# Moving ELU's sums and the residual of a graph attention layer from VectorE to GpSimd, with a second head's product moved the other way

## The chip, the cores and the metric

One Trainium2 chip, one core of it. A core has TensorE (matrix products into PSUM; PE in the profile, its weight loads PEld), VectorE (DVE), ScalarE (ACT), GpSimd (POOL) and SyncE (SP), which here only issues DMAs. The engines run side by side and wait for one another through semaphores. The metric is the device time of one execution in microseconds (us); lower is better.

## The reference

Two layers over 4096 nodes with 512 features. Layer 0 is dense attention with the adjacency matrix added to the logits. Layer 1 is graph attention with 8 heads of 64 features, and is the part that is edited:

```python
h = relu(layernorm(x))
nX = (h @ W).reshape(n, 8, 64).transpose(1, 0, 2)        # per head, then normalised over its 64 features
at1, at2 = nX . a1, nX . a2                              # one number per head and node
kg = leaky_relu(at1[i] + at2[j], 0.2) * adj[i, j]
attention = softmax(where(adj[i, j] != 0, kg, -32768), over j)
y = attention @ nX + nX
x = x + elu(y)
```

`elu(y)` is y where y is positive, and exp(y) - 1 elsewhere.

## The kernel before

Layer 0 runs first, to about 2090 us of the profile, and is not edited. Layer 1 works in groups: 8 chunks of 512 destination nodes i, times 2 halves of the heads (4 heads at a time), so 16 groups. A group has 32 steps, one for each block of 128 source nodes j; the 512 steps run in one loop, and the order of the instructions on every compute engine is written out by hand (`seq`). The DMA issues of SP that matter here are in that order too.

What one step n issues, in this order:

- `values(n - 4)`, TensorE, L996: the weighted sums of an earlier step, from the exponentials `t` into `acc` (PSUM), for 4 heads.
- `exponent(n - 3)`, ScalarE, L983: exp over the 4 heads of `t`, 2048 elements per partition.
- `leaky(n)`, VectorE: for two of the four heads a maximum and a sum from PSUM (L969 twice), for head 3 the product with the graph's values `g` (L973), and for heads 0 and 1 a sum with PSUM (L974).
- `weigh(n)`, GpSimd, L980: the product with `g` for the other three heads, 1536 elements per partition.
- `z_sums(n + 1)`, TensorE, L948 and L953: the logits of the next step, into PSUM tiles `d`, of which there are three.
- `relu(n + 1)`, ScalarE, L960: from PSUM to `t`.

`t` has six buffers. So GpSimd works on the step that VectorE has just left, or on an earlier one, and VectorE can run some steps ahead of it; the text calls this distance VectorE's lead.

SP issues the loads. Every fourth step `load_adj` brings `z2`, `nb` and `g` for the four steps after the running ones; `g` has two buffers, so its issue (L900) waits until GpSimd has finished the last product that read the older one, and everything behind it on SP waits too. `open_group` (L913, L916) loads `z1` and `u4` of the next group, four steps before that group begins, which puts it behind the `load_adj` of the same step. `load_rows` loads the residual `xi` and the rows `own` of a group at its step 12; there is one buffer of each.

The end of a group is spread over steps of the next one, counted from the step in which the group's last `values` run (`finish`): copies of `acc` on ScalarE at +0; transposes on TensorE at +1 and +2, each followed on VectorE by `divide` (L1027 to L1032), which also keeps the least and greatest sum in `low` and `high` for a flag at the very end; `minus` on ScalarE at +4 and +5; `exps` on ScalarE at +6 and +7; then, both on VectorE, `elu` (L1050) at +9 and `close` (L1054) at +10, which adds the residual and stores the result (L1058).

Of the kernel before, what the change touches and what calls it, by code (L numbers as in the profile page):

```python
# [10 lines left out]
F32 = mybir.dt.float32  # L11
# [7 lines left out]
P = 128  # L19
# [59 lines left out]
def fast_path(  # L79
# [45 lines left out]
    HB = HD + 1  # L125
    back = const.tile([P, 2, HB], F32, name="back")

    low = const.tile([P, 2, 4], F32, name="low")
    high = const.tile([P, 2, 4], F32, name="high")
    low0 = const.tile([P, SB], F32, name="low0")  # L130
    high0 = const.tile([P, SB], F32, name="high0")
    for t in (low, high, low0, high0):
        nc.vector.memset(t, 1.0)


# [742 lines left out]
    with tc.tile_pool(name="ga_in", bufs=2) as inputs, tc.tile_pool(  # L878
# [4 lines left out]
        JB = 4  # L883
        STEPS = [(ic, hg, jt) for ic in range(NI) for hg in range(NH // HG) for jt in range(NB)]
        n_steps = len(STEPS)
        loads, logits, zs, groups = {}, {}, {}, {}
        later = {}

        def load_adj(q):
# [19 lines left out]
        def open_group(n, queue):  # L909

            ic, hg, _ = STEPS[n]
            z1 = inputs.tile([P, GC], BF16, name="z1", tag="z1", bufs=2)
            seq(queue.dma_start(out=z1, in_=z1_d[:, hg, ts(ic, GC)]))  # L913
            u4 = inputs.tile([P, 2, GC], F32, name="u4", tag="u4", bufs=2)
            for e in range(2):
                seq(queue.dma_start(  # L916
                    out=u4[:, e, :].rearrange("p (b i) -> p b i", i=P),
                    in_=u4_d[ic * SB : (ic + 1) * SB, hg * HG + 2 + e, :]
                    .unsqueeze(0).to_broadcast([P, SB, P]),
                ))  # L920
            groups[ic, hg] = {"z1": z1, "u4": u4}
# [41 lines left out]
        def leaky(n):  # L963

            ic, hg, jt = STEPS[n]
            t, pair, u4 = logits[n], zs.pop(n), groups[ic, hg]["u4"]
            for e in (1, 0):
                h = hg * HG + 2 + e
                seq(nc.vector.scalar_tensor_tensor(  # L969
                    pair[1][:, 1, :] if e else t[:, 2, :], u4[:, e, :], at2m[:, jt, h : h + 1],  # L970
                    pair[1][:, e, :], ALU.max, ALU.add,
                ))
            seq(nc.vector.tensor_mul(t[:, 3, :], pair[1][:, 1, :], loads[n // JB][0][:, jt % JB, :]))  # L973
            seq(nc.vector.tensor_add(t[:, 0:2, :], t[:, 0:2, :], pair[0]))  # L974

        def weigh(n):

            g = loads[n // JB][0][:, STEPS[n][2] % JB, :].unsqueeze(1).to_broadcast([P, 3, GC])
            t = logits[n]
            seq(nc.gpsimd.tensor_mul(t[:, 0:3, :], t[:, 0:3, :], g))  # L980

        def exponent(n):
            seq(nc.scalar.activation(logits[n], logits[n], AF.Exp))  # L983
# [17 lines left out]
        def finish(n, ic, hg):  # L1001

            grp = groups.pop((ic, hg))
            ob = work.tile([P, 2, GC], F32, name="ob", tag="ob", bufs=1)
            y = work.tile([P, 2, SB * 2, HD], F32, name="y", tag="y", bufs=1)

            def room():
                grp["e"] = work.tile([P, 2, SB * 2, HD], F32, name="e", tag="ob", bufs=1)

            def copies():  # L1010
                for hf in range(2):
                    seq(nc.scalar.copy(ob[:, hf, :], grp["acc"][hf]))

            def to_rows(hf):
                pt = psum.tile([P, 2, GC], F32, name="pt1", tag="d", bufs=3)
                for b in range(SB):
                    col = (b % 2) * 2 * HB
                    seq(nc.tensor.matmul(  # L1018
                        pt[:, b // 2, col : col + 2 * HB], ob[:, hf, ts(b, P)],
                        back.rearrange("p e c -> p (e c)"), start=True, stop=True,  # L1020
                    ))
                grp["pt"] = pt[:, :, 0 : 4 * HB].rearrange("p k (q c) -> p k q c", c=HB)

            def divide(hf):
                v = grp.pop("pt")
                rinv = work.tile([P, 2, 4], F32, name="rinv1", tag="rinv1", bufs=2)
                seq(nc.vector.reciprocal(rinv, v[:, :, :, HD]))  # L1027
                seq(nc.vector.tensor_tensor(low, low, v[:, :, :, HD], ALU.min))
                seq(nc.vector.tensor_tensor(high, high, v[:, :, :, HD], ALU.max))
                v = v[:, :, :, 0:HD]  # L1030
                seq(nc.vector.tensor_mul(v, v, rinv.unsqueeze(3).to_broadcast([P, 2, 4, HD])))  # L1031
                seq(nc.vector.tensor_add(  # L1032
                    y[:, hf].rearrange("p (k q) e -> p k q e", k=2), v,
                    grp["own"][:, hf].rearrange("p b d -> p (b d)")
                    .rearrange("p (k q e) -> p k q e", k=2, e=HD),
                ))

            def flat(t):
                return t.rearrange("p f q e -> p (f q e)")

            def minus(hf):
                seq(nc.scalar.activation(grp["e"][:, hf], y[:, hf], AF.Relu, scale=-1.0))

            def exps(hf):
                e = grp["e"][:, hf]
                seq(nc.scalar.activation(e, e, AF.Exp, scale=-1.0))

            def elu():
                e = flat(grp["e"])
                seq(nc.vector.scalar_tensor_tensor(e, e, -1.0, flat(y), ALU.add, ALU.max))  # L1050

            def close():
                e = grp["e"]
                seq(nc.vector.tensor_add(  # L1054
                    flat(e), flat(e), grp["xi"].rearrange("p f b d -> p (f b d)")
                ))
                for f, ap in enumerate(pair_rows(out, ic, hg)):
                    nc.sync.dma_start(  # L1058
                        out=ap, in_=e[:, f].rearrange("p (b h) e -> p b (h e)", h=2)
                    )  # L1060

            for d, place, f in (
                (0, "mid", copies),
                (1, "mid", lambda: to_rows(0)), (1, "end", lambda: divide(0)),
                (2, "mid", lambda: to_rows(1)), (2, "end", lambda: divide(1)),
                (4, "end", room), (4, "end", lambda: minus(0)), (5, "end", lambda: minus(1)),
                (6, "end", lambda: exps(0)), (7, "end", lambda: exps(1)),
                (9, "end", elu), (10, "end", close),
            ):
                later.setdefault((n + d, place), []).append(f)  # L1070
# [34 lines left out]
        for n in range(n_steps + 15):  # L1105

            q = n // JB + 1
            if n == 1:
                store_rows(NI - 1, last_rows)
            if n % JB == (2 if q == NS - 1 else 0) and q < n_steps // JB:  # L1110
                load_adj(q)
                if q < NS:
                    load_features(q)
            if n < n_steps and STEPS[n][2] == 12:
                load_rows(n)
            if n + 4 < n_steps and STEPS[n + 4][2] == 0:
                open_group(n + 4, nc.sync)
            extra(n, "top")
            if 0 <= n - 4 < n_steps:
                values(n - 4)  # L1120
                if n % JB == 3:
                    loads.pop((n - 4) // JB)
                if STEPS[n - 4][2] == NB - 1:
                    finish(n, *STEPS[n - 4][:2])
            if 0 <= n - 3 < n_steps:
                exponent(n - 3)
            extra(n, "mid")
            for f in left.pop(n, []):
                f()
            if n % JB == 2 and n // JB < NS:  # L1130
                ones_in(n // JB)
            if n < n_steps:
                leaky(n)
                weigh(n)
            if n + 1 < n_steps:
                z_sums(n + 1)
                relu(n + 1)
            for f in left_late.pop(n, []):
                f()
            extra(n, "end")  # L1140
# [1 line left out]

        ends = work.tile([P, 4], F32, name="ends", tag="ends", bufs=1)
        nc.vector.tensor_reduce(ends[:, 0:1], low0, AX.X, ALU.min)
        nc.vector.tensor_reduce(ends[:, 1:2], low, AX.XY, ALU.min)
        nc.vector.tensor_reduce(ends[:, 2:3], high0, AX.X, ALU.max)
        nc.vector.tensor_reduce(ends[:, 3:4], high, AX.XY, ALU.max)
        good = work.tile([P, 4], F32, name="good", tag="good", bufs=1)
        nc.vector.tensor_scalar(good[:, 0:2], ends[:, 0:2], TINY, None, ALU.is_ge)
        nc.vector.tensor_scalar(good[:, 2:3], ends[:, 2:3], HUGE0, None, ALU.is_le)  # L1150
        nc.vector.tensor_scalar(good[:, 3:4], ends[:, 3:4], HUGE1, None, ALU.is_le)
        pl = psum.tile([4, P], F32, name="pl", tag="d", bufs=3)
        nc.tensor.transpose(pl, good, ident)
        worst = work.tile([4, 1], F32, name="worst", tag="worst", bufs=1)
# [409 lines left out]
```

## Time and profile before

| | |
|---|---|
| time, median of 3 runs | 4024.99 us (4022.72 to 4026.66) |
| the profiled execution | 4015.42 us, span 4013.6 us, mean clock of TensorE 0.982 |
| busy, share of the span | PE 95%, DVE 73%, ACT 44%, POOL 64% |
| GpSimd's product L980 | 512 instructions, 1783.5 us, 3517 ns each |
| VectorE's `elu` sum L1050 | 16, from 1226 to 6367 ns, median 1952 |
| VectorE's residual sum L1054 | 16, 1218 to 1232 ns |
| ScalarE's exponent L983 | 512 instructions, 974.4 us, 1903 ns each |

The shares are means over two layers with different limits: in layer 1 the product on GpSimd takes most of its time, in layer 0 GpSimd is idle for much of it. In the timeline, two columns of numbers stand ahead of the engine: the start and the duration; what stands in brackets at the end of a line is how long the engine was idle before it, and what ended that. A duration can overlap the next instruction's start by some 0.1 us, so the pace is read from start to start.

### The profile page before, as it was taken

What the parts mean: (1) busy time and instruction counts of PE and PEld (TensorE: products, weight loads), DVE (VectorE), ACT (ScalarE), POOL (GpSimd) and SP (SyncE); (2) the same over time, 40 slices, a digit from 0 to 9 for tenths busy, and PEclk for the clock granted to TensorE, in tenths of its full rate; (3) what the DMA queues carried; (4) which work ended last, traced back from release to release, by engine and by line L of the source; (5) the groups of instructions that cost most, each with busy time, mean ns of one, the idle gap of its engine ahead of it and who ended that gap; (6) DMA issues with size and microseconds to landing.
All of it is one profiled execution on the core that took longest, in us unless ns stands there. A gap on an engine that the chain in (4) does not pass through costs nothing. (4 is left out here: it accounts for less than half of the span.)

```text
span 4013.6 us, 43955 instructions
## 1 busy us (share of the span) xinstructions
PE 3810.1 (95%) x15217; PEld 1801.6 (45%) x15370; DVE 2921.6 (73%) x4425; ACT 1752.9 (44%) x1549; POOL 2552.0 (64%) x1249
## 2 busy tenths in 40 slices
PE   8989999999999999999988899999999999999997
PEld 4446666666666666666642222222222222222222
DVE  5445556565565656565556899999999999999997
ACT  1000011111111111111115787887778877877887
POOL 3432125252342525243357899999999999999998
PEclk9999999999999999999989999999999999999999
DMA  6466657667685857667565544444444444444442
GB/s 214 173 213 197 202 161 216 188 180 219 187 220 167 226 171 209 199 184 222 153 194 146 154 134 140 141 140 139 137 139 131 144 139 131 135 136 136 136 139 88
DMA packets 554407, 670.37 MB, mean 167 GB/s; under 512 B 79808, under 2 KB 397504, under 8 KB 534720
## 3 DMA queue, kind: packets, MB, share of 16 engines
q1 hardware_dynamic: 552112, 665.70, 55.7%
q8 instruction: 122, 2.00, 0.2%
q10 hardware_dynamic: 2064, 1.77, 0.2%
q14 instruction: 109, 0.89, 0.1%
HBM read 495.12 MB, written 172.23 MB: 166 GB/s over the span
## 5 line engine op out<-in xcount | busy, mean ns | idle before, releaser
L980 POOL TENSOR_TENSOR t<-t,g 128x1536 f32<-128x1536 f32 x512 | 1783.5, 3517 | 108.9 <-DVE t L974 85.4
L996 PE MATMUL acc<-t,nX 128*64 128x512 f32 x4096 | 1022.3, 621 | 20.3 <-ACT t L983 12.9
L739 POOL TENSOR_TENSOR total<-total,aT 128x512 f32<-128x512 f32 x248 | 339.7, 1370 | 1061.3 <-ACT aT L734 1054.8
L983 ACT ACTIVATE t<-t 128x2048 f32<-128x2048 f32 x512 | 974.4, 1903 | 3.0 <-POOL t L980 3.0
L749 PE MATMUL acc<-v,aT 128*128 128x512 f32 x2048 | 962.7, 593 | 0.0
L734 ACT ACTIVATE aT<-aT 128x512 f32<-128x512 f32 x256 | 161.2, 630 | 1325.0 <-DVE aT L729 1317.0
L960 ACT ACTIVATE t<-d 128x1024 f32<-128x1024 f32 x512 | 525.4, 1026 | 419.0 <-PE d L953 396.3
L974 DVE TENSOR_TENSOR t<-t,d 128x1024 f32<-128x1024 f32 x512 | 619.8, 1211 | 0.0
L953 PE MATMUL d<-nb,ident_b 128*128 128x512 bf16 x1895 | 521.3, 389 | 14.9 <-issue 9.4
L749 PEld LDWEIGHTS acc<-v,aT 128*128 128x128 f32 x2048 | 389.7, 190 | 273.8 <-issue 245.5
L996 PEld LDWEIGHTS acc<-t,nX 128*64 128x64 f32 x4096 | 254.9, 139 | 549.5 <-issue 360.0
L969 DVE SCALAR_TENSOR_TENSOR d<-u,at2m,d 128x512 f32<-128x512 f32 x512 | 383.7, 749 | 87.9 <-PE d L953 41.4
L969 DVE SCALAR_TENSOR_TENSOR t<-u,at2m,d 128x512 f32<-128x512 f32 x512 | 382.4, 747 | 55.2 <-DVE d L969 3.2
L729 DVE TENSOR_TENSOR aT<-aT,X 128x256 f32<-128x256 f32 x512 | 214.9, 420 | 279.2 <-PE X L721 275.8
L948 PE MATMUL d<-z,z 6*128 6x512 bf16 x2048 | 265.0, 388 | 115.6 <-DVE t L973 92.4
L729 DVE TENSOR_TENSOR aT<-aT,Z 128x256 f32<-128x256 f32 x384 | 159.6, 416 | 292.1 <-PE Z L721 287.5
L973 DVE TENSOR_TENSOR t<-d,g 128x512 f32<-128x512 f32 x512 | 349.9, 683 | 0.9 <-DMA g<-gT_d 0.9
L948 PEld LDWEIGHTS <-z 6*128 6x128 bf16 x2048 | 85.4, 91 | 539.6 <-issue 523.3
L713 DVE SCALAR_TENSOR_TENSOR gs<-ng,aT 128x512 f32<-128x512 bf16 x256 | 286.1, 1117 | 9.8 <-DMA gT_d<-gs 1.2
L721 PE MATMUL Z<-qt,hS 128*128 128x256 f32 x1024 | 265.9, 382 | 8.6 <-DVE aT L729 8.4
L953 PEld LDWEIGHTS <-ident_b 128*128 128x128 bf16 x2048 | 160.1, 98 | 246.8 <-issue 128.9
L721 PE MATMUL X<-qt,hT 128*128 128x256 f32 x1024 | 263.8, 380 | 0.5 <-DVE aT L729 0.5
(160 smaller groups left out, 3079.5 us busy)
## 6 DMA issues: line engine op xcount, KB each, us to landing
g<-gT_d SPq DMA_DIRECT2D x128, 1024.0 KB, 5.4
ag<-in_adj_dram SPq DMA_DIRECT2D x256, 256.0 KB, 5.6
hT<-h_d SPq DMA_DIRECT2D x64, 1024.0 KB, 5.9
hS<-s_d SPq DMA_DIRECT2D x64, 1024.0 KB, 8.2
gT_d<-gs SPq DMA_DIRECT2D x256, 256.0 KB, 3.1
nb<-nT_d SPq DMA_DIRECT2D x128, 512.0 KB, 3.3
nT_d<-ng SPq DMA_DIRECT2D x256, 128.0 KB, 3.4
z<-z_d SPq DMA_DIRECT2D x143, 128.0 KB, 2.1
```

Source lines behind the costliest of these rows:

```text
L721: seq(nc.tensor.matmul(out, a, b, start=start and k == 0, stop=k == 1, skip_group_check=not start,))
L729: seq(nc.vector.tensor_add(p, p, part))
L749: seq(nc.tensor.matmul(sums[ic][b], probs[s][:, ts(b, P)], v[:, jt, :], start=jt == 0, stop=jt == NB - 1))
L948: seq(nc.tensor.matmul(pair[hh // 2][:, hh % 2, :], z2[rows, ts(jt % JB, P)], groups[ic, hg]["z1"][rows, :], start=True, stop=False,))
L953: seq(nc.tensor.matmul(pair[hh // 2][:, hh % 2, :], ident_b, ng[:, jt % JB, :], start=False, stop=True))
L960: seq(nc.scalar.activation(t[:, 0:2, :], zs[n][0], AF.Relu, scale=4.0))
L969: seq(nc.vector.scalar_tensor_tensor(pair[1][:, 1, :] if e else t[:, 2, :], u4[:, e, :], at2m[:, jt, h : h + 1], pair[1][:, e, :], ALU.max ...
L973: seq(nc.vector.tensor_mul(t[:, 3, :], pair[1][:, 1, :], loads[n // JB][0][:, jt % JB, :]))
L974: seq(nc.vector.tensor_add(t[:, 0:2, :], t[:, 0:2, :], pair[0]))
L980: seq(nc.gpsimd.tensor_mul(t[:, 0:3, :], t[:, 0:3, :], g))
L983: seq(nc.scalar.activation(logits[n], logits[n], AF.Exp))
L996: seq(nc.tensor.matmul(grp["acc"][hf][ts(e, HD), :], nX[jt // SB][:, jt % SB, hg * HG + 2 * hf + e, :], t[:, 2 * hf + e, :], start=jt == 0 ...
```

## The change

Five things are edited, all in layer 1.

1. `elu` and `close` run on GpSimd. Since GpSimd only adds there, ScalarE prepares both terms: `positive` makes y its positive part after `exps(0)` at +6, and `less_one` subtracts one from the exponentials at +8.
2. In the steps +9 and +10 of 15 groups (the set `light`; the last group has no products left to share) VectorE takes the product of heads 2 and 3, and GpSimd that of heads 0 and 1 alone.
3. `open_group` runs ten steps ahead of a group rather than four.
4. `divide` writes its reciprocals into one tile that is kept, `inverses`, and no longer updates `low` and `high`; the flag is worked out from `inverses` at the end.
5. The tile `inverses` is declared twice; the first declaration is not used.

```diff
+        inverses = gat.tile([P, NI, 2, 2, 2, 4], F32, name="inverses")
+        light = {n + d for n in range(NB + 3, n_steps, NB) for d in (9, 10)}
...
+            mine = 2 if n in light else 1
             for e in (1, 0):
                 h = hg * HG + 2 + e
                 seq(nc.vector.scalar_tensor_tensor(
-                    pair[1][:, 1, :] if e else t[:, 2, :], u4[:, e, :], at2m[:, jt, h : h + 1],
-                    pair[1][:, e, :], ALU.max, ALU.add,
+                    pair[1][:, e, :] if e > 1 - mine else t[:, 2, :], u4[:, e, :],
+                    at2m[:, jt, h : h + 1], pair[1][:, e, :], ALU.max, ALU.add,
                 ))
-            seq(nc.vector.tensor_mul(t[:, 3, :], pair[1][:, 1, :], loads[n // JB][0][:, jt % JB, :]))
+            g = loads[n // JB][0][:, jt % JB, :].unsqueeze(1).to_broadcast([P, mine, GC])
+            seq(nc.vector.tensor_mul(t[:, HG - mine : HG, :], pair[1][:, 2 - mine : 2, :], g))
...
         def weigh(n):
-            g = loads[n // JB][0][:, STEPS[n][2] % JB, :].unsqueeze(1).to_broadcast([P, 3, GC])
+            mine = 2 if n in light else 3
+            g = loads[n // JB][0][:, STEPS[n][2] % JB, :].unsqueeze(1).to_broadcast([P, mine, GC])
             t = logits[n]
-            seq(nc.gpsimd.tensor_mul(t[:, 0:3, :], t[:, 0:3, :], g))
+            seq(nc.gpsimd.tensor_mul(t[:, 0:mine, :], t[:, 0:mine, :], g))
...
-                rinv = work.tile([P, 2, 4], F32, name="rinv1", tag="rinv1", bufs=2)
+                rinv = inverses[:, ic, hg, hf]
                 seq(nc.vector.reciprocal(rinv, v[:, :, :, HD]))
-                seq(nc.vector.tensor_tensor(low, low, v[:, :, :, HD], ALU.min))
-                seq(nc.vector.tensor_tensor(high, high, v[:, :, :, HD], ALU.max))
...
+            def positive():
+                seq(nc.scalar.activation(flat(y), flat(y), AF.Relu))
+            def less_one():
+                seq(nc.scalar.add(flat(grp["e"]), flat(grp["e"]), -1.0))
             def elu():
                 e = flat(grp["e"])
-                seq(nc.vector.scalar_tensor_tensor(e, e, -1.0, flat(y), ALU.add, ALU.max))
+                seq(nc.gpsimd.tensor_add(e, e, flat(y)))
             def close():
                 e = grp["e"]
-                seq(nc.vector.tensor_add(
+                seq(nc.gpsimd.tensor_add(
                     flat(e), flat(e), grp["xi"].rearrange("p f b d -> p (f b d)")
                 ))
...
-                (6, "end", lambda: exps(0)), (7, "end", lambda: exps(1)),
+                (6, "end", lambda: exps(0)), (6, "end", positive), (7, "end", lambda: exps(1)),
+                (8, "end", less_one),
                 (9, "end", elu), (10, "end", close),
...
-            if n + 4 < n_steps and STEPS[n + 4][2] == 0:
-                open_group(n + 4, nc.sync)
+            if n + 10 < n_steps and STEPS[n + 10][2] == 0:
+                open_group(n + 10, nc.sync)
```

More of the change, by code (lines that the diff above doesn't have):

```diff
@@ L126, in fast_path @@
     back = const.tile([P, 2, HB], F32, name="back")
-    low = const.tile([P, 2, 4], F32, name="low")
-    high = const.tile([P, 2, 4], F32, name="high")
     low0 = const.tile([P, SB], F32, name="low0")
     high0 = const.tile([P, SB], F32, name="high0")
-    for t in (low, high, low0, high0):
+    for t in (low0, high0):
         nc.vector.memset(t, 1.0)
@@ L885, in fast_path @@
         n_steps = len(STEPS)
+        inverses = gat.tile([P, NI, 2, 2, 2, 4], F32, name="inverses")
+        inverses = gat.tile([P, NI, 2, 2, 2, 4], F32, name="inverses")
         loads, logits, zs, groups = {}, {}, {}, {}
+        light = {n + d for n in range(NB + 3, n_steps, NB) for d in (9, 10)}
         later = {}
@@ L1144, in fast_path @@
         nc.vector.tensor_reduce(ends[:, 0:1], low0, AX.X, ALU.min)
-        nc.vector.tensor_reduce(ends[:, 1:2], low, AX.XY, ALU.min)
+        of_all = inverses.rearrange("p i g f k q -> p (i g f k q)")
+        nc.vector.tensor_reduce(ends[:, 1:2], of_all, AX.X, ALU.max)
         nc.vector.tensor_reduce(ends[:, 2:3], high0, AX.X, ALU.max)
-        nc.vector.tensor_reduce(ends[:, 3:4], high, AX.XY, ALU.max)
+        nc.vector.tensor_reduce(ends[:, 3:4], of_all, AX.X, ALU.min)
         good = work.tile([P, 4], F32, name="good", tag="good", bufs=1)
-        nc.vector.tensor_scalar(good[:, 0:2], ends[:, 0:2], TINY, None, ALU.is_ge)
+        nc.vector.tensor_scalar(good[:, 0:1], ends[:, 0:1], TINY, None, ALU.is_ge)
+        nc.vector.tensor_scalar(good[:, 1:2], ends[:, 1:2], 1.0 / TINY, None, ALU.is_le)
         nc.vector.tensor_scalar(good[:, 2:3], ends[:, 2:3], HUGE0, None, ALU.is_le)
-        nc.vector.tensor_scalar(good[:, 3:4], ends[:, 3:4], HUGE1, None, ALU.is_le)
+        nc.vector.tensor_scalar(good[:, 3:4], ends[:, 3:4], 1.0 / HUGE1, None, ALU.is_ge)
         pl = psum.tile([4, P], F32, name="pl", tag="d", bufs=3)
```

## The prediction

> **What bounds the kernel now.** I read the page's shares first, then the stretches of layer 1 group by group, then GpSimd's waits, then VectorE, TensorE and SyncE in time around one group's end. The mean shares mislead: they mix layer 0 (to about 2090 us) with layer 1, the rest, and only layer 1 is edited.
>
> ```profile
> 2996.20:3112.46 116.26, 108.07 (x523) 33.03 (x530) 107.23 (x142) 93.11 (x71) 111.82 (x33) 0.99 0.43 137
> 3112.46:3226.10 113.64, 106.46 (x520) 32.94 (x528) 107.12 (x141) 93.11 (x71) 111.75 (x33) 1.00 0.45 140
> 2417.15:3928.80 1511.65, 1413.97 (x6746) 430.70 (x6868) 1401.37 (x1822) 1210.42 (x911) 1456.05 (x421) 0.98 0.44 138
> ```
>
> These are stretches: length, then busy time of PE, PEld, DVE, ACT and POOL. The first two are one group (32 steps) each, cut at the residual sum; the third is thirteen groups, 116.28 us each. GpSimd (POOL) is busiest: 112 us in each group, idle 55.6 us over thirteen, 4.2 us a group. So it is nearly the limit, and its idle time is what can be had without making it faster. Who makes it idle:
>
> ```profile
> POOL t L980 <- DVE t L974: 85.4, 60, 4.4
> DVE d L969 <- DMA u<-u_d: 36.1, 14, 3.5
> PE d L948 <- DVE t L973: 77.7, 51, 6.0
> ```
>
> (The last row is from the steady window of layer 1.) VectorE delivers late, and itself waits 2.6 us at 14 group starts for u4. Now one undisturbed step, and the disturbed ones of the group at 2412 to 2533 us:
>
> ```profile
> 2434.55 0.75 DVE L969 SCALAR_TENSOR_TENSOR t<-u,at2m,d 128x512 f32<-128x512 f32 x1
> 2435.22 0.68 DVE L973 TENSOR_TENSOR t<-d,g 128x512 f32<-128x512 f32 x1
> 2435.82 1.21 DVE L974 TENSOR_TENSOR t<-t,d 128x1024 f32<-128x1024 f32 x1
> 2437.84 44.55 POOL L980 TENSOR_TENSOR t<-t,g 128x1536 f32<-128x1536 f32 x13
> 2469.73 1.43 SPq L916 DMA_DIRECT2D u<-u_d  x2
> 2478.71 0.76 DVE L969 SCALAR_TENSOR_TENSOR d<-u,at2m,d 128x512 f32<-128x512 f32 x1 [2.73 <-DMA u<-u_d]
> 2483.09 2.72 PE L996 MATMUL acc<-t,nX 128*64 128x512 f32 x8
> 2513.90 1.94 PE L996 MATMUL acc<-t,nX 128*64 128x512 f32 x8 [0.24 <-ACT t L983]
> 2526.72 1.95 DVE L1050 SCALAR_TENSOR_TENSOR e<-e,y 128x1024 f32<-128x1024 f32 x1
> 2530.84 0.39 PE L948 MATMUL d<-z,z 6*128 6x512 bf16 x2 [1.55 <-DVE t L973]
> 2531.83 1.22 DVE L1054 TENSOR_TENSOR e<-e,xi 128x1024 f32<-128x1024 f32 x1
> 2532.13 3.36 PE L996 MATMUL acc<-t,nX 128*64 128x512 f32 x8
> ```
>
> VectorE and TensorE repeat every 3.245 us (L969 at 2433.70 and 2436.95). GpSimd repeats every 3.43 us (44.55/13). So VectorE gains 0.19 us of lead per step, 6.1 us in 32, and loses it at the group's end: two divides 3.85 us (2.17 and 1.68), ELU 1.87, residual 1.15, the u4 wait 2.6, and TensorE slow after each gap (acc 2.72 or 3.36 us instead of 1.94). With the lead gone, GpSimd waits.
>
> **What the Trainium skill says.** Its page "SBUF — State Buffer", section "SBUF: two separate sides": a VectorE instruction with two SBUF inputs and a GpSimd one exclude each other on a shared port. The trace agrees: L1050 takes 1.95 us beside GpSimd (5.4 to 6.4 in three of sixteen groups) and 1.23 at the end, where GpSimd is done, and the product beside L1050 or L1054 takes 4.38 instead of 3.44. Other VectorE work of a step reads PSUM, and shows no such stretch. The Trainium skill's "TensorE: Matmul & The Clock Gate", section "What's actually happening": idleness halves TensorE's clock for a while. The trace agrees and is stricter: a gap of 1.55 us was enough (the lines at 2530.84 and 2532.13), one of 0.53 was not.
>
> **The change, part by part.**
>
> *GpSimd.* In 30 steps (15 groups, two each) its product shrinks from 1536 to 1024 elements, and one 1024-element sum follows. A 1024-element operation is not in the trace; from 1.27 us (L351, 512) and 3.44 (1536) it is 2.35 us. The Trainium skill's "GPSIMD Engine Reference", section 3.1, measures 4497 ns at 2048, which halves to 2.25 (estimate). I take 2.35, bounds 2.25 and 2.45. A group costs 30 x 3.437 + 4 x 2.35 = 112.5 us, plus 2.6 where L351 and L352 run. Against 32 x 3.437 = 110.0 that is 2.5 more, but the port conflict of L1050 and L1054 (0.94 each, 1.9 a group) goes.
>
> *VectorE.* Off: 1.87 + 1.15 of sums, L1028 and L1029 (0.1 us of each divide's chain at most, 0.2 a group). On: the 1024-wide product, priced as L974 (1.21) against L973 (0.68), 0.53 twice. That releases the PSUM buffer 0.53 us later, so TensorE's next z slips about 0.36, but VectorE has its own 1.13 us add in between.
>
> *u4 and z1 ten steps ahead.* Three DMA issues move on SP from behind g of step 28 (it waits for GpSimd's product of step 27) to behind g of step 20. The data land in 7.9 us and now have ten steps, 34 us. Both buffers have been free since the group before. SP's other issues slip by at most the 1.9 us that the three take, at a step where z and nb have four steps. So 2.6 us of wait and the clock loss behind it (1.35: L969 waits of 0.32 and 1.03) go. Bounds: all gone, or g of the next group becomes the next wait, issued at 2468.77 for step 32, landing in 5.4, leaving 1 us.
>
> *ScalarE.* Two more 1024-element operations a group: relu of y after step +6, minus one after +8 (counted from the step in which the group's last values run). By L1042 (0.62 at 512) and L983 (1.90 at 2048) one is 1.05, or 0.95 behind another; the Trainium skill's "ScalarE: Activation LUTs", section "What ACT_TABLE_LOAD costs", gives 1.04 by its formula. What is queued behind: exponent (L983), then TensorE's values (L996). An extra of 0.52 now stalls L996 by 0.24 (the line at 2513.90), so the slack is 0.28. Before: four such stalls, 0.96. After: 0.24 x 3, then 1.47 - 0.28 = 1.19 at +6 and 0.67 at +8: 2.58, 1.6 more. If the 1.19 gap slows TensorE's clock, 1.4 on top (3.36 - 1.94).
>
> *New waits.* GpSimd's ELU sum waits for ScalarE's minus one, issued a step earlier: hidden by the product ahead of it. The residual sum now ends when GpSimd gets there; SP's xi load waits for it, and behind it stand out's stores, z, nb and g. g waits for a later product on GpSimd anyway, and z and nb land 7.4 us after it for a use 15 us minus VectorE's lead (under 6) later. Nothing.
>
> *Sum.* VectorE with TensorE needs 32 x 3.245 + 2.07 + 1.58 (divides) + 1.06 + 2.58 + 0.3 (copies of acc) = 111.4 us, below GpSimd's 112.5. GpSimd then sets the pace; I leave it 0.4 us of idle time a group. Thirteen groups: 13 x 112.9 + 2 x 2.6 = 1472.9 against 1511.65: -38.8. The group before them (123.15 us, GpSimd idle 7.5): 115.1 + 1.6 = 116.7: -6.4. The first group and layer 0: nothing. At the very end no product hides the last group's work: 0.95 + 0.95 on ScalarE, and two sums at 2.35 instead of 1.23: +4.2. The reduces over the kept reciprocals end under it. Total -41.0, span 3972.6.
>
> The timed runs lie 9 to 13 us above this span (its own execution took 4015.42). The 5.4 us sums, if more frequent there, would explain part and vanish. I keep 9.4 of the median's 11.4: **3982 us**.
>
> **Rivals.**
> 1. *ScalarE's extras slow TensorE's clock* (for: 1.55 us did; against: gaps of 1.10 and 1.49 us at the kernel's end did not). Two slow spells and a follow-up, 3 us: VectorE's side becomes 114.4, so 13 x 114.8 = 1492.4, -19; with -5 and +4.2, about 4003.
> 2. *Slower:* the same chain loses so much that GpSimd keeps its idle time and has the longer work as well. It decides where ScalarE's delay passes 116.3 - 111.4 = 4.9 us beyond the stalls counted. At 6 us: 117.4 x 13 = +15, tail +4: about 4042. Against it: ScalarE is busy only 93 of 116 us, and the lead absorbs a single stall.
> 3. *The inputs come early but g is late instead*, or the idle time returns elsewhere: gains eaten by the added 2.5 us: about 4024, no change. Little for it: VectorE waited for g once, 0.9 us.
>
> **Numbers.** Main case 0.66 (own range 3968 to 3996), rival 1 0.22, rival 2 0.08, rival 3 0.04. A difference under 0.2% (8 us) could not be told from no change here. Faster 0.88, same 0.04, slower 0.08. The floor is GpSimd without any idle time and no offset kept: about 3966. The range goes from there to 4008, past rival 1.
>
> **What would show it.** Right: GpSimd's idle time in thirteen groups falls from 55 us to about 5; groups of 112.5 to 113.5; no L969 wait for u; 1024-wide sums of 2.35 us; the end about 4 us longer. Wrong: groups of 115 or more with GpSimd waiting for the add of leaky; L996 waiting over 1 us for ScalarE with acc at 3 us behind it; VectorE waiting for g; sums far off 2.35.

## The result, and the profile after

The changed kernel takes 3966.09 us (median of 4 runs, 3965.83 to 3967.40) against 4025.82 us (4022.72 to 4030.26) beside it: a ratio of 0.9867, with a 95% interval of 0.9848 to 0.9886. Its span is 3964.2 us, 49.4 us shorter than the one before.

The row of GpSimd's product on the page before, then on the page after, with the slices of GpSimd's busy time after:

```profile
L980 POOL TENSOR_TENSOR t<-t,g 128x1536 f32<-128x1536 f32 x512 | 1783.5, 3517 | 108.9 <-DVE t L974 85.4
```

```profile
POOL 3432225243242525234256999999999999999998
L985 POOL TENSOR_TENSOR t<-t,g 128x1536 f32<-128x1536 f32 (+1 forms) x512 | 1724.0, 3440 | 47.6 <-DVE t L978 26.9
```

The idle time before the product fell from 108.9 to 47.6 us, and what is left stands at the start of layer 1 (20.6 us for the first nX and 26.9 for VectorE, all of it before the steady groups). Two groups in steady state, in the same columns as before (length, then PE, PEld, DVE, ACT and POOL busy):

```profile
2982.50:3094.57 112.07, 105.97 (x519) 32.23 (x528) 105.97 (x135) 95.89 (x73) 112.07 (x36) 1.00 0.45 142
3094.57:3206.64 112.07, 106.39 (x520) 32.29 (x528) 106.00 (x135) 95.84 (x73) 112.07 (x35) 1.00 0.45 142
```

GpSimd is busy in every microsecond of a group; TensorE's clock is at 1.00. The waits in layer 1 have turned round: ScalarE now waits for GpSimd, and neither u nor VectorE holds anything up.

```profile
ACT t L988 <- POOL t L985: 81.6, 161, 1.1
POOL t L985 <- DVE t L978: 4.3, 2, 2.2
```

The moved work itself, in the group at 2640 us. L1059 is ELU's sum and L1063 the residual, both on GpSimd now; L977 is VectorE's product, here two heads wide; L985 is GpSimd's product, L988 ScalarE's exponent and L1001 TensorE's `values`:

```profile
2626.59 1.94 PE L1001 MATMUL acc<-t,nX 128*64 128x512 f32 x8 [1.41 <-ACT t L988]
2631.07 1.23 DVE L977 TENSOR_TENSOR t<-d,g 128x1024 f32<-128x1024 f32 x1
2639.06 2.39 POOL L1059 TENSOR_TENSOR e<-e,y 128x1024 f32<-128x1024 f32 x1
2641.38 2.40 POOL L985 TENSOR_TENSOR t<-t,g 128x1024 f32<-128x1024 f32 x1
2643.73 2.39 POOL L1063 TENSOR_TENSOR e<-e,xi 128x1024 f32<-128x1024 f32 x1
```

From start to start a 1024-element operation of GpSimd takes 2.33 us, and VectorE's wider product 1.23 instead of 0.68. TensorE waits 1.41 us for ScalarE at +6, and its acc right after takes 1.94 us, as without a wait.

Where the 49.4 us are, read from the starts of GpSimd's products (the first is product 0): the thirteen groups from product 78 to 494 went from 1512.0 to 1462.3 us (-49.7); what lies ahead of them gained 3.7; the end, after the last of them, lost 3.9. In the thirteen groups GpSimd's idle time fell by 55.8 us, to 0.2, and its busy time rose by 6.1, to 1462.2.

A number that the rest of the text uses is VectorE's lead: the start of a product on GpSimd less the end of VectorE's add for the same step, a mean over ten groups.

| kernel | at step 31 | at step 32, the group's first | GpSimd idle, us a group |
|---|---|---|---|
| before | 3.0 | 0.5 | 4.2 |
| after | 5.4 | 5.4 | 0.0 |

### The profile page after: what moved, and what is told of

Read it like the earlier page. It is cut to its first block, busy times and chain, and to the rows that moved or that the text cites. A ratio compares the mean times of both kernels' runs of the same rounds, so it can differ in the third digit from the quotient of the medians.

```text
span 3964.2 us, 43905 instructions
## 1 busy us (share of the span) xinstructions
PE 3774.4 (95%) x15217; PEld 1789.4 (45%) x15370; DVE 2890.3 (73%) x4328; ACT 1797.0 (45%) x1581; POOL 2564.4 (65%) x1281
## 5 line engine op out<-in xcount | busy, mean ns | idle before, releaser
L985 POOL TENSOR_TENSOR t<-t,g 128x1536 f32<-128x1536 f32 (+1 forms) x512 | 1724.0, 3440 | 47.6 <-DVE t L978 26.9
L1001 PE MATMUL acc<-t,nX 128*64 128x512 f32 x4096 | 996.3, 607 | 72.1 <-ACT t L988 58.0
L988 ACT ACTIVATE t<-t 128x2048 f32<-128x2048 f32 x512 | 975.8, 1906 | 87.7 <-POOL t L985 86.6
L1001 PEld LDWEIGHTS acc<-t,nX 128*64 128x64 f32 x4096 | 250.5, 136 | 597.6 <-issue 340.9
L972 DVE SCALAR_TENSOR_TENSOR d<-u,at2m,d 128x512 f32<-128x512 f32 x542 | 407.3, 752 | 51.9 <-PE d L955 31.1
L972 DVE SCALAR_TENSOR_TENSOR t<-u,at2m,d 128x512 f32<-128x512 f32 x482 | 360.0, 747 | 50.0 <-DVE d L972 0.9
L977 DVE TENSOR_TENSOR t<-d,g 128x512 f32<-128x512 f32 (+1 forms) x512 | 366.3, 715 | 4.3 <-DMA g<-gT_d 1.4
L950 PE MATMUL d<-z,z 6*128 6x512 bf16 x2048 | 252.2, 386 | 45.5 <-DVE t L977 22.7
L950 PEld LDWEIGHTS <-z 6*128 6x128 bf16 x2048 | 76.8, 91 | 456.0 <-issue 451.9
L719 PE MATMUL X<-qt,hS 128*128 128x256 f32 x1024 | 263.9, 381 | 0.0
```

The source lines that it names most:

```text
L719: seq(nc.tensor.matmul(out, a, b, start=start and k == 0, stop=k == 1, skip_group_check=not start,))
L972: seq(nc.vector.scalar_tensor_tensor(pair[1][:, e, :] if e > 1 - mine else t[:, 2, :], u4[:, e, :], at2m[:, jt, h : h + 1], pair[1][:, e, ...
L977: seq(nc.vector.tensor_mul(t[:, HG - mine : HG, :], pair[1][:, 2 - mine : 2, :], g))
L985: seq(nc.gpsimd.tensor_mul(t[:, 0:mine, :], t[:, 0:mine, :], g))
L1001: seq(nc.tensor.matmul(grp["acc"][hf][ts(e, HD), :], nX[jt // SB][:, jt % SB, hg * HG + 2 * hf + e, :], t[:, 2 * hf + e, :], start=jt == 0 ...
```

## The experiments

Theory A was the prediction's: VectorE's extra work and waits add up, and GpSimd is idle where the sum is more than it gives. I set it against theory B, that only the moved sums count. The kernel before was timed again beside each set of runs, with medians from 4011 to 4026 us; the ratios, and the lengths of groups in the profiles, are therefore surer than the times.

**Early inputs alone, on the kernel before.**

```diff
-            if n + 4 < n_steps and STEPS[n + 4][2] == 0:
-                open_group(n + 4, nc.sync)
+            if n + 10 < n_steps and STEPS[n + 10][2] == 0:
+                open_group(n + 10, nc.sync)
```

> The kernel before with the early group inputs alone (z1 and u4 ten steps ahead). Theory A (a budget of lead): VectorE with TensorE needs 116.1 us a group before, of which the u4 wait and the slow clock after it are 3.95; without them 112.2, next to GpSimd's 110.0 plus 1.9 of port conflict. So groups of 112.5 us, no wait for u, GpSimd idle under 1 us a group: about 3970 us, most of the whole gain. Theory B (moving the sums is what counts, and u4's wait only comes back elsewhere): groups of about 115, 4005 us or more.

Measured: 4008.56 us, a ratio of 0.9977 (0.9961 to 0.9993). Theory A fails here, and the time that theory B named holds: the wait for u is gone, and almost nothing is won. GpSimd is still idle 4.3 us a group, but elsewhere: before, 3.3 of it lay in steps 0 to 6 of a group (u's wait and the divides) and 1.0 in steps 13 to 15, behind ELU's sum (+9 is step 12 of the next group); now all of it lies in steps 13 to 15. The views are the ELU sum's durations (least, median, greatest, in ns), GpSimd's timeline and VectorE's:

```profile
L1050 DVE SCALAR_TENSOR_TENSOR e<-e,y x16: 1226/5666/8281, 2294.1 to 4000.2; 128x1024 f32<-128x1024 f32 x16
```

```profile
3089.03 20.56 POOL L980 TENSOR_TENSOR t<-t,g 128x1536 f32<-128x1536 f32 x6
3114.00 7.84 POOL L980 TENSOR_TENSOR t<-t,g 128x1536 f32<-128x1536 f32 x2 [4.41 <-DVE t L974]
```

```profile
3105.01 5.67 DVE L1050 SCALAR_TENSOR_TENSOR e<-e,y 128x1024 f32<-128x1024 f32 x1
3110.60 0.74 DVE L969 SCALAR_TENSOR_TENSOR d<-u,at2m,d 128x512 f32<-128x512 f32 x1
```

The median sum went from 1.95 to 5.67 us. The one at 3105.01 starts while GpSimd has a running product and a ready one behind it. Both finish first, at 3109.59; the sum ends 1.1 us later (alone it takes 1.23 in all); VectorE then needs 3.3 us for the next step, and GpSimd stands still for 4.41. So such a sum waits until GpSimd runs out of work: with one product ready behind the running one it took 5.5 to 7.9 us, with two 8.28. Eleven of the fifteen sums beside products went this way, against three in the kernel before. VectorE's mean lead just ahead of the sum is 1.4 us here and was 0.75; that the lead decides how many sums go this way is not shown.

**The moved sums with the inputs four steps ahead.** The same two lines, turned back in the changed kernel.

> The changed kernel with the group inputs four steps ahead again. Theory A: VectorE's side gets 3.95 us a group back, 111.4 + 3.95 = 115.3 at most, GpSimd idle 1 to 3 us a group: 3985 to 4010 us. Theory B: the lead now swallows the wait, GpSimd idle under 0.5 us a group: within 8 us of 3966.

Measured: 4031.18 us (4025.74 to 4037.08), a ratio of 1.0042 (1.0025 to 1.0059), so a little slower than before, and above both theories. SP, VectorE, TensorE and GpSimd around a group's start:

```profile
2698.66 0.36 SPq L902 DMA_DIRECT2D g<-gT_d  x1
2700.02 1.15 SPq L918 DMA_DIRECT2D u<-u_d  x2
2709.02 0.76 DVE L972 SCALAR_TENSOR_TENSOR d<-u,at2m,d 128x512 f32<-128x512 f32 x1 [5.52 <-DMA u<-u_d]
2713.62 3.66 PE L1001 MATMUL acc<-t,nX 128*64 128x512 f32 x8
2721.59 10.31 POOL L985 TENSOR_TENSOR t<-t,g 128x1536 f32<-128x1536 f32 x3 [1.86 <-DVE t L978]
```

u is issued 1.4 us after GpSimd's product of step 27 ends (2698.63), because g ahead of it on SP waits for that product. It lands 9 us on. GpSimd needs 13.7 us for the four products between; VectorE needs 3.3 us after u for its first step. So VectorE begins each group with 0.2 us of lead (5.3 at the step before), however far ahead it was: the wait grew from 2.6 to 5.4 us. GpSimd is then idle 4.2 us a group, 1.1 of it in the first three steps, 2.2 at the divides and 0.9 at the first of the wider steps, and it is busy 0.7 us a group longer than before.

**Four steps ahead, but ahead of g.** Against the run above, this changes only the place in SP's order.

```diff
+            if n + 4 < n_steps and STEPS[n + 4][2] == 0:
+                open_group(n + 4, nc.sync)
             if n % JB == (2 if q == NS - 1 else 0) and q < n_steps // JB:
                 load_adj(q)
...
-            if n + 4 < n_steps and STEPS[n + 4][2] == 0:
-                open_group(n + 4, nc.sync)
```

> The changed kernel with the group inputs four steps ahead again, but issued ahead of that step's z, nb and g instead of behind them. Theory A (the inputs are pinned to GpSimd: they stand on SP behind g, which waits for GpSimd's product of step 27, so whatever lead VectorE has is cut to about half a microsecond at each group's start): the lead survives, no wait for u, GpSimd never idle, within 8 us of 3966. Theory B (what counts is the distance of four steps against ten): the wait for u stays, about 4030 us.

Measured: 3966.99 us (3964.46 to 3969.77), the changed kernel's time; the ratio is 0.9884 (0.9868 to 0.9901), and the thirteen groups take 1461.8 us against its 1462.3. On SP, u now stands ahead of g:

```profile
2680.31 1.36 SPq L918 DMA_DIRECT2D u<-u_d  x2
2681.77 0.51 SPq L894 DMA_DIRECT2D z<-z_d  x1
2682.38 0.38 SPq L898 DMA_DIRECT2D nb<-nT_d  x1
2693.05 0.36 SPq L902 DMA_DIRECT2D g<-gT_d  x1
```

The lead is 5.3 us at step 31 and 5.3 at step 32, and GpSimd is never idle. The distance in steps is that of the run before; what mattered is the issue of g, which waits 10 us for GpSimd and no longer holds u up.

**Both sums back on VectorE, in the changed kernel.**

```diff
-        light = {n + d for n in range(NB + 3, n_steps, NB) for d in (9, 10)}
+        light = {n + d for n in range(NB + 3, n_steps, NB) for d in ()}
...
-                seq(nc.gpsimd.tensor_add(e, e, flat(y)))
+                seq(nc.vector.tensor_add(e, e, flat(y)))
...
-                seq(nc.gpsimd.tensor_add(
+                seq(nc.vector.tensor_add(
```

> The changed kernel with both sums back on VectorE (as plain adds, ScalarE still prepares the terms) and GpSimd on three heads in every step. Theory A: VectorE's side about 113 us a group (two adds of 1.15 on, two wider products off), GpSimd 110.0 plus 1.9 of conflict: 3972 to 3980 us, and the products of GpSimd beside the adds take 4.4 us instead of 3.44. Theory B: back to 4000 us or more.

Measured: 4005.79 us, 0.9971 (0.9962 to 0.9979). Theory A misses by 26 us; theory B's time holds. GpSimd is idle 3.9 us a group, and a plain add meets the same conflict as the fused one:

```profile
L1059 DVE TENSOR_TENSOR e<-e,y x16: 1218/4896/7695, 2295.3 to 3995.9; 128x1024 f32<-128x1024 f32 x16
```

**The conflict without the port.** Theory C says that what costs is the shared port. To test it, the kernel before, with the inputs ten steps ahead, gets two reductions in place of the sums: VectorE work of the same length that reads one SBUF tensor. This kernel leaves out ELU's last sum and the residual. Theory D is that VectorE's work itself costs, whatever it reads.

```diff
-                seq(nc.vector.scalar_tensor_tensor(e, e, -1.0, flat(y), ALU.add, ALU.max))
+                part = work.tile([P, 16], F32, name="part", tag="part", bufs=2)
+                seq(nc.vector.tensor_reduce(part, e.rearrange("p (a b) -> p a b", a=16), AX.X, ALU.add))
...
-                seq(nc.vector.tensor_add(
-                    flat(e), flat(e), grp["xi"].rearrange("p f b d -> p (f b d)")
+                part = work.tile([P, 16], F32, name="part", tag="part", bufs=2)
+                seq(nc.vector.tensor_reduce(
+                    part, grp["xi"].rearrange("p f b (c d) -> p (f b c) d", c=2), AX.X, ALU.add
                 ))
```

> The kernel before with early group inputs, and with the two sums of each group replaced on VectorE by two reductions over as many elements of one SBUF input (leaves out ELU's last sum and the residual; the exponentials are stored). Theory C (a sum with two SBUF inputs loses the shared port to products of GpSimd that are already queued, and the more lead VectorE has the longer it waits): about 1.2 us for each reduction, no stretch of GpSimd's product to 4.4 us, GpSimd hardly idle, groups of 110.5 to 112.5 us, 3945 to 3970 us. Theory D (VectorE's work itself is what costs): 4000 us or more, like the kernel with the sums.

Measured: 3934.30 us (3929.98 to 3939.25), a ratio of 0.9801 against 0.9977 with the sums, so some 70 us below, and 11 below the range that I gave. Each reduction takes 1.21 us beside GpSimd's products, and GpSimd is idle 0.6 us a group:

```profile
L1051 DVE TENSOR_REDUCE part<-e x16: 1210/1212/1219, 2293.2 to 3926.2; 128x16 f32<-128x1024 f32 x16
```

Theory C holds, D falls: 2.4 us of VectorE work a group could be had for next to nothing. A reduction also writes less than a sum (16 numbers per partition for 1024), but writing is not what costs: the add of `leaky` (L974 in the kernel before), with one input in PSUM and one in SBUF, also writes 1024, and takes 1.21 to 1.22 us in all 512 steps beside the same products. That leaves the second SBUF input.

**No second head on VectorE.** `for d in ()` in `light` alone.

> The changed kernel without the second head on VectorE: GpSimd has three heads in every step and the two sums as well. If GpSimd sets the pace: groups of 32 x 3.43 + 2 x 2.33 = 114.4 us, 2.2 more in 15 groups, about 3999 us and still no idle time on GpSimd. If VectorE shares the limit: less than 20 us longer.

Measured: 3999.46 us; groups of 114.2 us against 112.1, idle 0.0. GpSimd sets the pace, and each step in which a head moves is worth 1.1 us.

**Four wider steps a group.** `for d in (9, 10, 20, 21)`.

> The changed kernel with two more steps of each group (after +20 and +21) in which VectorE takes a second head. If VectorE with TensorE has the slack that GpSimd's waits on no one suggest: groups of 112.1 - 2.2 = 109.9 us, about 3934 us. If VectorE with TensorE needs 111.4 us as reckoned, plus 1.06: groups of 112 to 113 us, 3960 to 3980 us, with GpSimd idle again.

Measured: 3953.30 us, between the two: groups of 111.55 us, and GpSimd waits for VectorE again:

```profile
2834.45 20.59 POOL L985 TENSOR_TENSOR t<-t,g 128x1536 f32<-128x1536 f32 x6 [0.59 <-DVE t L978]
2855.97 2.38 POOL L985 TENSOR_TENSOR t<-t,g 128x1024 f32<-128x1024 f32 x1 [0.93 <-DVE t L978]
```

So VectorE with TensorE is the limit at 111.55; without the two further products, at 0.53 each, it would need about 110.5 us, an estimate from this group, where the prediction had 111.4.

**The two running extremes again, on top of that.** The two lines of `divide` that update `low` and `high` come back, and the flag is worked out from these.

> The changed kernel with four wider steps a group, in which VectorE is the limit (groups of 111.55 us), and with the two running extremes in every divide again. If they cost what their place in the chain shows, 0.1 us each divide: 0.2 us in 16 groups, 3 us more than 3953. If they cost their full busy time (0.11 + 0.16): 0.54 a group, 8 us more. If nothing: the same.

Measured: 3955.01 us; groups of 111.75 us, 0.2 more. Each pair costs 0.1 us of the chain, as its place shows. In the changed kernel itself, where GpSimd has no idle time, the kept reciprocals should then be worth nothing; no run tests that.

**ScalarE's additions in halves.** With four wider steps, `positive` and `less_one` are cut in two. The sums, and the first two wider steps, move to +12 and +13, and the rows are loaded at step 17. The order of the end of a group:

```diff
-                (6, "end", lambda: exps(0)), (6, "end", positive), (7, "end", lambda: exps(1)),
-                (8, "end", less_one),
-                (9, "end", elu), (10, "end", close),
+                (6, "end", lambda: exps(0)), (7, "end", lambda: exps(1)),
+                (8, "end", lambda: positive(0)), (9, "end", lambda: positive(1)),
+                (10, "end", lambda: less_one(0)), (11, "end", lambda: less_one(1)),
+                (12, "end", elu), (13, "end", close),
```

> The same four wider steps, with ScalarE's two new operations cut into halves over four steps (after +8 to +11), the sums and their wider steps at +12 and +13, and the rows loaded at step 17. ScalarE's extras then stall TensorE by 0.24 us in eight steps, 1.9 us a group, where the undivided ones show 1.4 at +6 and 0.7 at +8 beside three of 0.24, 2.8: groups of 110.5 to 110.9 us, 3938 to 3945 us. If ScalarE isn't what VectorE's side loses: 3953.

Measured: groups of 110.8 us, as expected, but 3947.59 us in time (3943.32 to 3953.07), a little above the range. In its profile, the slowest of the four executions, layer 1 began 4.7 us later than with four wider steps alone, ahead of the edit, and what follows the last product is 1.9 us longer. TensorE's waits for ScalarE are short ones now:

```profile
2858.64 1.94 PE L1001 MATMUL acc<-t,nX 128*64 128x512 f32 x8 [0.25 <-ACT t L988]
2865.36 1.94 PE L1001 MATMUL acc<-t,nX 128*64 128x512 f32 x8 [0.25 <-ACT t L988]
```

They fell from 1.43 to 1.08 us a group (means of ten groups), by less than the 0.9 that I expected; so they explain only part of the 0.8 us by which a group became shorter.

**The last group's sums on VectorE**, on top of the halves. ScalarE's two operations are left out for that group.

```diff
+            last = n >= n_steps
...
+                if last:
+                    seq(nc.vector.scalar_tensor_tensor(e, e, -1.0, flat(y), ALU.add, ALU.max))
+                else:
+                    seq(nc.gpsimd.tensor_add(e, e, flat(y)))
...
+                seq((nc.vector if last else nc.gpsimd).tensor_add(
```

> As the one with halves, and the last group's sums on VectorE as in the kernel before, without ScalarE's two operations there, since GpSimd has no products left beside it: the end is 4 us shorter, 3934 to 3941 us.

Measured: 3942.63 us (3940.54 to 3945.95), 0.9814 (0.9790 to 0.9839): 5 us below the one without, 1.6 us above the range. What follows the last product is 4.2 us shorter in its profile (21.1 against 25.3), as expected. It is the fastest kernel here that computes all of the reference.

**The kernel before, once more.**

> The kernel before once more, for a second profile. If the 10 us by which its timed runs exceed the first profile's span come from ELU sums that wait long for the shared port, a profile with a longer span shows more than three sums above 5 us, and one of 4013 us about three. If they come from elsewhere, the number of long sums doesn't follow the span.

Measured: 4020.30 us (4005.44 to 4038.30), a profile of 4009.2 us in which no sum takes over 3.2 us (three took over 5 in the first, of 4013.6). One more profile with fewer long sums and a shorter span fits the idea, but proves little, and this profile's span is at the low end of its own timed runs. What stretches those to 4038 is open.

## Why the prediction was right, point by point

- **GpSimd at its limit, with idle time to remove.** Right. It is never idle in the steady groups. I had left it 0.4 us a group (0 measured) and priced its work at 112.5 us (112.1 measured: 2.33 instead of 2.35 for a short operation, 3.425 instead of 3.437 for a long one). Over thirteen groups these two terms are 10 to 11 us, as much as -38.8 fell short of -49.7. The gain of the group before them was put too high: -6.4 against -3.7.
- **The end.** +4.2 predicted, +3.9 measured.
- **The step from span to time.** I kept 9.4 us for the timed runs; 1.9 was measured. In every profiled execution the time is 1.8 us above the span; the rest of the 11.4 before was that the profiled execution (4015.42) was faster than the timed ones, while those of the changed kernel lie within 1.6 us of one another. This term is 7.5 of the 16 us between 3982 and 3966; the thirteen groups, less what the group before them fell short, are most of the other 8.4. The measured time lies on the floor that the prediction gave for GpSimd without idle time and without offset, at the very edge of the range and 2 us outside the main case's own: the mechanism was right, the sizes were too cautious in one direction.
- **VectorE's side.** 111.4 was about 0.9 too high (110.5 by the kernel with four wider steps). ScalarE's waits alone were put 1.1 too high: 2.58 us priced, 1.43 measured in that kernel. The lead never ran out in the steady groups: 0.6 us at its lowest, in the first wider step (+9).
- **ScalarE.** The wait at +6 was priced at 1.19 us and is 1.19 to 1.41; the clock did not fall after it in any steady group, so rival 1 did not come. Its ground was weaker than the prediction took it to be: of ten gaps of 1.52 to 1.55 us in the kernel before, four were followed by a slow acc, like the one that the prediction shows, and six were not.
- **The failed step.** "So 2.6 us of wait and the clock loss behind it (1.35) go", as terms of a sum. The parts don't add: alone the early inputs are worth -0.23%, the moved sums with the late inputs +0.42%, together -1.33%. The late input is pinned to GpSimd's progress and takes whatever lead there is (3.0 us before, 5.3 after the sums are moved). And the port conflict, which I priced at 1.9 us a group on GpSimd, also leaves GpSimd idle for 4.4 us after each sum that waits for all its ready work: three in fifteen before, eleven with the early inputs. The prediction had seen the three long sums and gave them no price. Each of the two uses up what removing the other would give. It was luck that this did no harm to the number: the change makes both edits at once.
- **Rival 2**, slower, was not what the change did; its outcome came in the kernel without the early inputs, by another mechanism than ScalarE.

## What to carry to other kernels

A lead between two engines is a stock, not a sum of costs: look for the wait that sets it back to zero (here a load that stands on a queue behind an issue that waits for the slower engine) before you make the faster engine faster. Test both halves of a change alone; two that each do nothing may be worth 1.3% together. Work with two SBUF inputs was better kept off VectorE beside a GpSimd that had the next instruction ready; a reduction of the same length was nearly free there.

## What was not expected of the hardware

The Trainium skill's "SBUF — State Buffer", section "SBUF: two separate sides", has the loser of the shared port block for the other's whole instruction. The traces agree: all ELU sums that met a running product (59 of 60 in four profiles: the kernel before twice, with the early inputs, and with the sums back on VectorE) end 1.1 to 1.2 us after the end of a product, however long they waited. So a sum waits for a product to end and then runs its own time. In the short case this is the running product, and the next one then takes 4.4 us instead of 3.44, as if it waited in its turn. For the sum of the kernel before at 2526.72, which takes 1.95 us, the views of GpSimd show the running product and the next:

```profile
2524.12 3.46 POOL L980 TENSOR_TENSOR t<-t,g 128x1536 f32<-128x1536 f32 x1
2527.55 4.42 POOL L980 TENSOR_TENSOR t<-t,g 128x1536 f32<-128x1536 f32 x1
```

In the long case the next product goes first, and so does each that is ready behind it: the sum takes 4.9 to 8.3 us. What was not expected is that a waiting sum can lose more than once. Which of the two goes first wasn't settled: in the kernel before, sums that started 2.6 us into a product went both ways (twelve of 1.95 us, two of 5.4), and with the early inputs those that started 2.1 to 2.5 us into one all took the long way.

In the kernel before and in the one with the moved sums and the late inputs, TensorE's acc took 2.4 to 3.7 us instead of 1.94 after most gaps of over 2 us and, in the first, after four of the ten of 1.52 to 1.55; it took 1.94 after each gap of up to 1.41 in the steady groups of the changed kernel.
